# Output projection moved ahead of the last attention unit, residual in a ring of three, q added on GpSimd, ScalarE's order written by hand

## The chip, the cores and the metric

One core of one Trainium2 chip. The time is the device time of one execution in microseconds (us), the median of several. Where two kernels are compared, they ran in turn on the same chip; before had medians of 4112 to 4136 us in five sets of runs, so ratios and not times are compared across sets.

## The reference

Two layers over 32 batches of 512 tokens by 512 features, all float32. The first is attention with 8 heads of 64 under a sparse adjacency mask, the second a graph attention layer over the same mask.

```python
h = relu(layernorm(x));  q, k, v = h @ Wq + bq, h @ Wk + bk, h @ Wv + bv     # 8 heads of 64
attn = softmax(q @ k.T / 8 + (1 - adj) * -1e9);  x = x + (attn @ v) @ Wo + bo
h = relu(layernorm(x));  g = h @ W                                             # layer 2
e = leaky_relu(g @ a[:512] + (g @ a[512:]).T, 0.2) * adj
x = x + elu(softmax(e) @ g + beta * g)
```

## The kernel before

A step of the loop works on four batches at once. Its parts, by letters: units 0 to 3 of the attention of one batch (two heads each: the scores of this unit and the values and sums of the unit before it), V, K, Q, W the four projections (W is the product with Wo), U the combinations of the attention's output oT that W needs (uT), D the sums and diagonal of the second layer's softmax, G its gather, Y its final product, N the transposes of the next batch's normalised x, R the load of the residual.

```python
order = {...}.get(b, "0VDU1G2YNR3WKQ")
```

A projection is done in seven products of quarter size (Strassen's scheme in Winograd's form) and not eight; q is the second of them, and is added to two of the four quarters of the result (abridged: the `yield`s are left out; `one` and `two` are the evictions, which read a finished quarter out of PSUM).

```python
def seven(name, w, B, tokens, one, two):
    ...
    x_ = tile1("x");  times(x_, A11, "b11", True)            # times: sixteen matmuls, 128x256
    y_ = tile1("y");  nc.scalar.copy(y_, x_)
    qz = psum.tile([P, 2, N], F32, ...);  z_ = qz[:, 1, :]
    times(qz[:, 0, :], S1, "t1", True)
    q_ = wtile([P, N], f"q5_{name}", "q5", 1)
    nc.scalar.copy(q_, qz[:, 0, :])                           # q to SBUF
    times(y_, S2, "t2", False, onto=True)
    nc.scalar.copy(z_, y_)                                    # z starts from y
    times(x_, A12, "b21", False, onto=True);   one(0, 0, x_)
    times(z_, S3, "t3", False, onto=True);     two(1, 1, z_, q_)
    times(y_, S4, "b22", False, onto=True);    two(0, 1, y_, q_)
    times(z_, NA22, "t4", False, onto=True);   one(1, 0, z_)
```

TensorE's, VectorE's and GpSimd's order is that of the program text; ScalarE's is found by the compiler. VectorE's work that has time is put into a list with a time from which it may run and a cost; after each TensorE block the program's own clock says what fits.

```python
def pe(us):
    clock["pe"] += us
    while True:
        for i, (key, ready, cost, fn) in enumerate(spare):
            if max(clock["dve"], ready) + cost <= clock["pe"] + 0.4:
                spare.pop(i); clock["dve"] = max(clock["dve"], ready) + cost; fn(); break
        else:
            return

def later(key, wait, cost, fn):
    spare.append((key, max(clock["dve"], clock["pe"]) + wait, cost, fn))
```

On this list are: the statistics and normalisation of the batch that N turns one step later (`norm0`, `x` below; "the next batch's" from here on), the reciprocal of the softmax sums (`rd`), the statistics and dot products of the second layer (of its normalised input `hn`), and the four rows `at` of its softmax. `need(key)` forces what is left of a kind. W adds to the residual:

```python
def add(i, k, p):
    r = x1[k][:, :, ts(i, H)]
    nc.vector.scalar_tensor_tensor(r, quarter(p), 1.0 / VS, r, op0=ALU.mult, op1=ALU.add)
def two(i, k, p, r):
    add(i, k, p)
    add(i, k, r)                     # q, from SBUF
    ...
```

## Time and profile before

| | before |
|---|---|
| median of 3 runs | 4135.91 us (4128.72 to 4138.94) |
| profiled execution | 4131.9 us, granted clock 0.959 |
| one steady step | 126.2 us; 110.9 if TensorE never waited |

TensorE is busy most of the time, so what counts is how much longer each part of a step takes than its matmuls need. A line of the timeline gives start, duration, engine, line, operation, output and inputs, shapes, number. The prediction shows the lines of V, where most is lost.

```profile
2041.62 3.61 PE L502 MATMUL po<-e,v 128*64 128x512 f32 x16
...
2048.60 5.01 PE L472 MATMUL ps<-qT,kT 64*128 64x512 f32 x16
```

The sixteen matmuls of the values take 3.6 us. The sixteen of the scores take 5.0, after the 2.02 us wait for `rd` that the prediction shows.

### The profile page before, as it was taken

The page shows a single profiled execution, that of the slowest core. Times are in us where ns is not written, and L with a number is a line of the kernel's source. Part 1 is how long each engine was busy: PE and PEld are TensorE (multiplying, and loading weights), DVE is VectorE, ACT ScalarE, POOL GpSimd, SP SyncE. Part 2 cuts the span into 40 slices and gives each one's busy share as a digit, 9 for nine tenths or more (in the row PEclk, how much of TensorE's full clock was granted, in tenths as well). Part 3 has the DMA queues.
Part 4 walks back from the last instruction along what each step waited for, and adds up shares of the span by engine and source line. Part 5 has one row for each costly group of instructions (what it writes and reads, how often), then busy time and mean ns, then how long its engine had stood idle before and what let it go on. Part 6 is the DMA issues. An engine that isn't in the chain of part 4 may idle for free. (4 is left out here: it accounts for less than half of the span.)

```text
span 4131.9 us, 59288 instructions
## 1 busy us (share of the span) xinstructions
PE 3762.2 (91%) x24402; PEld 1812.2 (44%) x24402; DVE 2500.7 (61%) x3577; ACT 1400.9 (34%) x2086; POOL 2178.4 (53%) x1762
## 2 busy tenths in 40 slices
PE   8899999999999999999999999999999998999976
PEld 5344444444444444444444444444344444444422
DVE  5566655566656666556666556665556665666563
ACT  3333333333333333333333333333333333333321
POOL 5545556455565455564555644655545556545542
PEclk9899999999999999999999999999999999999988
DMA  3001101001101011010001010111000110101010
GB/s 106 23 3 34 34 31 34 12 25 34 34 31 34 4 34 34 32 34 9 28 34 34 31 34 4 34 34 34 31 17 21 34 34 31 34 4 34 24 33 24
DMA packets 71604, 120.86 MB, mean 29 GB/s; under 512 B 12384, under 2 KB 16480, under 8 KB 71328
## 3 DMA queue, kind: packets, MB, share of 16 engines
q1 hardware_dynamic: 69872, 115.18, 8.8%
q8 instruction: 193, 3.16, 0.3%
q0 software_dynamic: 368, 0.79, 0.1%
q10 hardware_dynamic: 1088, 1.05, 0.1%
q14 instruction: 83, 0.68, 0.1%
HBM read 83.37 MB, written 33.63 MB: 28 GB/s over the span
## 5 line engine op out<-in xcount | busy, mean ns | idle before, releaser
L482 DVE TENSOR_TENSOR e<-ps,nmT 128x1024 f32<-128x1024 f32 x384 | 456.8, 1217 | 667.7 <-PE ps L472 667.6
L493 POOL TENSOR_TENSOR es<-e,e 128x512 f32<-128x512 f32 x256 | 335.4, 1333 | 768.3 <-ACT e L486 768.3
L493 POOL TENSOR_TENSOR es<-es,e 128x512 f32<-128x512 f32 x512 | 693.8, 1387 | 0.0
L486 ACT ACTIVATE e<-e 128x1024 f32<-128x1024 f32 x512 | 541.3, 1057 | 411.0 <-DVE e L482 368.2
L472 PE MATMUL ps<-qT,kT 64*128 64x512 f32 x2048 | 513.8, 644 | 2.7 <-DVE e L482 2.7
L502 PE MATMUL po<-e,v 128*64 128x512 f32 x2048 | 464.2, 594 | 0.4 <-ACT e L486 0.2
L522 DVE RECIPROCAL rd<-pd 128x512 f32<-128x512 f32 x128 | 428.9, 3351 | 41.5 <-POOL oT L525 41.5
L46 PE MATMUL pg<-at,hn 128*64 128x512 f32 x2048 | 449.9, 597 | 4.4 <-DVE dmax L645 2.2
L46 PE MATMUL py<-w,gT 128*64 128x512 f32 x2048 | 446.4, 594 | 0.0
L525 POOL TENSOR_TENSOR oT<-oT,rd 128x512 f32<-128x512 f32 x128 | 168.3, 1315 | 332.4 <-DVE rd L522 332.4
L472 PEld LDWEIGHTS ps<-qT,kT 64*128 64x128 f32 x2048 | 199.7, 202 | 325.7 <-issue 234.2
L283 POOL TENSOR_TENSOR rs<-rs,mhalf 128x2 f32<-128x2 f32 (+1 forms) x96 | 87.6, 913 | 424.8 <-DVE rs L282 392.6
L46 PE MATMUL qz_v<-wv,tT 128*64 128x256 f32 x1024 | 170.8, 493 | 145.7 <-ACT qz_v L387 145.7
L46 PEld LDWEIGHTS pg<-at,hn 128*64 128x64 f32 x2048 | 146.0, 138 | 303.2 <-issue 276.7
L46 PEld LDWEIGHTS py<-w,gT 128*64 128x64 f32 x2048 | 145.1, 137 | 296.9 <-issue 247.6
L502 PEld LDWEIGHTS po<-e,v 128*64 128x64 f32 x2048 | 141.2, 137 | 250.8 <-issue 233.8
L675 POOL TENSOR_TENSOR y<-y,x 128x512 f32<-128x512 f32 x128 | 167.7, 1319 | 158.0 <-DVE y L673 101.6
L672 DVE TENSOR_SCALAR y<-y 128x512 f32<-128x512 f32 x128 | 100.0, 781 | 246.6 <-ACT y L671 246.6
L515 ACT COPY oT<-po 128x512 f32<-128x512 f32 x128 | 74.4, 581 | 514.0 <-PE po L502 514.0
L509 PE MATMUL pd<-es,ones 128*64 128x512 f32 x512 | 151.6, 650 | 78.0 <-DVE rd L522 69.4
L424 POOL TENSOR_TENSOR qT<-qT,edge 128x256 f32<-128x256 f32 x128 | 91.6, 737 | 188.0 <-DVE qT L420 188.0
L671 ACT ACTIVATE y<-py,rd 128x512 f32<-128x512 f32 x128 | 87.9, 687 | 284.7 <-PE py L46 216.6
(180 smaller groups left out, 5939.7 us busy)
## 6 DMA issues: line engine op xcount, KB each, us to landing
x<-in_x_dram SPq DMA_DIRECT2D x128, 256.0 KB, 2.9
x<-in_x_dram SPq DMA_DIRECT2D x64, 512.0 KB, 4.4
out_dram<-y SPq DMA_DIRECT2D x128, 256.0 KB, 2.3
s<-row_s SPq DMA_DIRECT2D x32, 256.0 KB, 3.7
adj<-in_adj_dram SPq DMA_DIRECT2D x4, 256.0 KB, 7.8
w<-in_L_gnn_W_dram SPq DMA_DIRECT2D x1, 1024.0 KB, 7.8
wk<-in_L_gnn_Wk_dram ACTq DMA_DIRECT2D x3, 256.0 KB, 5.0
wq<-in_L_gnn_Wq_dram SPq DMA_DIRECT2D x3, 256.0 KB, 6.4
```

The costliest lines, as they stand in the source:

```text
L46: nc.tensor.matmul(out[s : s + HD], lhsT[:, s : s + HD], rhs, start=start, stop=stop, skip_group_check=onto)
L424: nc.gpsimd.tensor_tensor(qh, qh, edge8[:, ts(k, H)], op=ALU.mult)
L472: nc.tensor.matmul(ps[s], st["kT"][j][rows, ts(k, P)], st["qT"][j][rows, :], start=True, stop=True)
L482: nc.vector.tensor_tensor(e, p, nmT[:, k, :].unsqueeze(1).to_broadcast([P, 2, N]), op=ALU.add)
L486: nc.scalar.activation(e, e, AF.Exp)
L493: nc.gpsimd.tensor_tensor(es[:, s, :], one[:, s, :], e[:, s, :], op=ALU.add)
L502: nc.tensor.matmul(po[s * HD : (s + 1) * HD, :], v[k // 2][:, k % 2, (2 * j + s) * HD : (2 * j + s + 1) * HD], e[k][:, s, :], start=k == 0 ...
L509: nc.tensor.matmul(pd[s * HD : (s + 1) * HD, :], ones[:, :HD], st["es"][j][:, s, :], start=True, stop=True)
L522: nc.vector.reciprocal(rd, st["pd"])
L525: nc.gpsimd.tensor_tensor(o, o, rd, op=ALU.mult)
L672: nc.vector.tensor_scalar(y, y, 1.0, -1.0, op0=ALU.min, op1=ALU.add)
L675: nc.gpsimd.tensor_tensor(y, y, st["x1"][t // 2][:, t % 2, :], op=ALU.add)
```

## The change

Four things at once: W goes ahead of unit 3, so that its results are there sooner; the residual, which W needs, is loaded in two halves at different places, the first ahead of Y, in a ring of three buffers used in turn (paid for by a ring of three in place of four for the attention's output oT); q is added on GpSimd, not VectorE; ScalarE's order is taken from the text, with a second list (`ends`) for ScalarE and GpSimd work that follows deferred VectorE work. Some waits and costs of the list were adjusted too.

```diff
-BY_HAND = {mybir.EngineType.PE, mybir.EngineType.DVE, mybir.EngineType.Pool}
+BY_HAND = {
+    mybir.EngineType.PE, mybir.EngineType.DVE, mybir.EngineType.Pool, mybir.EngineType.Activation,
+}
 ...
+    def then(key, fn):
+        ends.append((key, clock["dve"], fn))      # done by pe() once clock["pe"] + 0.4 has reached it
 ...
-        nc.scalar.copy(q_, qz[:, 0, :])
+        nc.scalar.activation(q_, qz[:, 0, :], AF.Copy, scale=scale)
+        if more:
+            more(q_)
 ...
-            st["o"].append(pair(b, "oT", j // 2, "oP", 4))
+            st["o"].append(pair(b, "oT", j // 2, "oP", 3))
 ...
-    def residual(b, st, tag="x1", bufs=2):            # both halves
+    def residual(b, st, i, tag="x1", bufs=3):         # half i
 ...
             add(i, k, p)
-            add(i, k, r)
 ...
+        def more(q_):
+            for i in (1, 0):
+                r = x1[1][:, :, ts(i, H)]
+                nc.gpsimd.tensor_tensor(r, r, quarter(q_), op=ALU.add)
 ...
-                    later(key, 1.5 + i, 0.7, lambda t=t, g=g, r=r: third(t, g, r))
+                        later(key, 1.2 + i, 0.8, lambda t=t, g=g, r=r: third(t, g, r))
 ...
-            later(("at", b), 5.5, 1.45, lambda k=k: rest(k))
+            later(("at", b), 4.5, 1.6, lambda k=k: rest(k))
 ...
-        norm0(b, states[b]["x"], *((30.0, 10.0) if b > 1 else (6.0, 2.0)))
+        norm0(b, states[b]["x"], *((36.0, 6.0) if b > 1 else (6.0, 2.0)))
 ...
-        }.get(b, "0VDU1G2YNR3WKQ")
+        }.get(b, "0VDU1G2rYNRW3KQ")                   # r: first half of the residual, R: second
```

(The exponential of the last scores, the exponentials and sums of `at`, the ReLUs of `hn` and what follows `rd` are moved into functions given to `then`.)

More of the change, by code (lines that the diff above doesn't have):

```diff
@@ L149, with run_spare @@
     clock = {"pe": 0.0, "dve": 0.0}
-    spare = []
+    spare, ends = [], []
+    def run_spare(i):
+        _, ready, cost, fn = spare.pop(i)
+        clock["dve"] = max(clock["dve"], ready) + cost
+        fn()
     def pe(us):
         clock["pe"] += us
+        till = clock["pe"] + 0.4
         while True:
-            for i, (key, ready, cost, fn) in enumerate(spare):
-                if max(clock["dve"], ready) + cost <= clock["pe"] + 0.4:
-                    spare.pop(i)
-                    clock["dve"] = max(clock["dve"], ready) + cost
-                    fn()
-                    break
+            fits = [i for i, (_, t, cost, _) in enumerate(spare) if max(clock["dve"], t) + cost <= till]
+            due = [i for i, (_, t, _) in enumerate(ends) if t <= till]
+            if due:
+                ends.pop(due[0])[2]()
+            elif fits:
+                run_spare(fits[0])
             else:
@@ L171, in later @@
         spare.append((key, max(clock["dve"], clock["pe"]) + wait, cost, fn))
+    def then(key, fn):
+        ends.append((key, clock["dve"], fn))
     def need(key):
-        while any(k == key for k, *_ in spare):
-            i = next(i for i, (k, *_) in enumerate(spare) if k == key)
-            _, ready, cost, fn = spare.pop(i)
-            clock["dve"] = max(clock["dve"], ready) + cost
-            fn()
+        while True:
+            mine = [i for i, e in enumerate(ends) if e[0] == key]
+            todo = [i for i, e in enumerate(spare) if e[0] == key]
+            if mine:
+                ends.pop(mine[0])[2]()
+            elif todo:
+                run_spare(todo[0])
+            else:
+                return
     adj_sb = []
@@ L354, in turn, with seven @@
         st["hT"] = combos(b, "tT", h)
-    def seven(name, w, B, tokens, one, two):
+    def seven(name, w, B, tokens, one, two, scale=1.0, more=None):
         def times(p, a, bl, start, onto=False):
@@ L485, in scores, with rest @@
             dve(1.2)
-        nc.scalar.activation(e, e, AF.Exp)
         st["e"][j].append(e)
-        if k == 1:
-            st["es"][j] = wtile([P, 2, N], f"es_{b}_{j}", "es", 1)
-        if k:
-            one, es = (st["e"][j][0] if k == 1 else st["es"][j]), st["es"][j]
-            for s in range(2):
-                nc.gpsimd.tensor_tensor(es[:, s, :], one[:, s, :], e[:, s, :], op=ALU.add)
+        def rest():
+            nc.scalar.activation(e, e, AF.Exp)
+            if k == 1:
+                st["es"][j] = wtile([P, 2, N], f"es_{b}_{j}", "es", 1)
+            if k:
+                one, es = (st["e"][j][0] if k == 1 else st["es"][j]), st["es"][j]
+                for s in range(2):
+                    nc.gpsimd.tensor_tensor(es[:, s, :], one[:, s, :], e[:, s, :], op=ALU.add)
+        if k < T - 1:
+            rest()
+        else:
+            then("e", rest)
     def values(b, j, st):
         need("rd")
+        need("e")
         po = st["po"] = psum.tile([P, N], F32, name=f"po_{b}_{j}", tag="po")
@@ L522, in divide, with rest @@
             nc.vector.reciprocal(rd, st["pd"])
-            junk = wtile([P, N], f"rj_{b}_{j}", "rj", 1, BF16)
-            nc.scalar.activation(junk, rd, AF.Copy, accum_out=rsum[:, b, j : j + 1])
-            nc.gpsimd.tensor_tensor(o, o, rd, op=ALU.mult)
-        later("rd", 0.0, 3.4, divide)
-    def residual(b, st, tag="x1", bufs=2):
-        st["x1"] = []
-        for i in range(2):
-            r = pair(b, "x1", i, tag, bufs)
-            nc.sync.dma_start(r, x[b, ts(i, H), :].rearrange("(t p) f -> p t f", p=P))
-            for t in range(2):
-                nc.gpsimd.tensor_tensor(r[:, t, :], r[:, t, :], c_row, op=ALU.add)
-            st["x1"].append(r)
+            def rest():
+                junk = wtile([P, N], f"rj_{b}_{j}", "rj", 1, BF16)
+                nc.scalar.activation(junk, rd, AF.Copy, accum_out=rsum[:, b, j : j + 1])
+                nc.gpsimd.tensor_tensor(o, o, rd, op=ALU.mult)
+            then("rd", rest)
+        later("rd", 0.0, 3.4, divide)
+    def residual(b, st, i, tag="x1", bufs=3):
+        r = pair(b, "x1", i, tag, bufs)
+        nc.sync.dma_start(r, x[b, ts(i, H), :].rearrange("(t p) f -> p t f", p=P))
+        for t in range(2):
+            nc.gpsimd.tensor_tensor(r[:, t, :], r[:, t, :], c_row, op=ALU.add)
+        st["x1"].append(r)
     def out_proj(b, st):
@@ L556, in two @@
             add(i, k, p)
-            add(i, k, r)
             if i == 0:
                 norm1(b, st, (2, 3))
-        return seven(f"w{b}", wo, st["oT"], True, one, two)
+        def more(q_):
+            for i in (1, 0):
+                r = x1[1][:, :, ts(i, H)]
+                nc.gpsimd.tensor_tensor(r, r, quarter(q_), op=ALU.add)
+        return seven(f"w{b}", wo, st["oT"], True, one, two, 1.0 / VS, more)
     def norm1(b, st, rows):
@@ L579, in second, with rest @@
             nc.vector.scalar_tensor_tensor(nb, mv[:, :, 0], -1.0, rstd, op0=ALU.mult, op1=ALU.mult)
-            for i, t in enumerate(rows):
-                hn = wtile([P, D], f"hn_{b}_{t}", "hn", 4)
-                nc.scalar.activation(
-                    hn, st["x1"][t // 2][:, t % 2, :], AF.Relu,
-                    bias=nb[:, i : i + 1], scale=rstd[:, i : i + 1],
-                )
-                st["hn"][t] = hn
-                for g, r in ((0, wa1_r), (1, wa2_r)):
-                    later(key, 1.5 + i, 0.7, lambda t=t, g=g, r=r: third(t, g, r))
+            def rest():
+                for i, t in enumerate(rows):
+                    hn = wtile([P, D], f"hn_{b}_{t}", "hn", 4)
+                    nc.scalar.activation(
+                        hn, st["x1"][t // 2][:, t % 2, :], AF.Relu,
+                        bias=nb[:, i : i + 1], scale=rstd[:, i : i + 1],
+                    )
+                    st["hn"][t] = hn
+                    for g, r in ((0, wa1_r), (1, wa2_r)):
+                        later(key, 1.2 + i, 0.8, lambda t=t, g=g, r=r: third(t, g, r))
+            then(key, rest)
         def third(t, g, r):
@@ L614, in rest, with summed @@
             nc.vector.scalar_tensor_tensor(z, z, ALPHA, z, op0=ALU.mult, op1=ALU.max)
-            nc.scalar.activation(z, z, AF.Exp)
             st["at"].append(z)
-            if k == 1:
-                st["as"] = wtile([P, N], f"as_{b}", "as", 1)
-                nc.gpsimd.tensor_tensor(st["as"], st["at"][0], z, op=ALU.add)
-            elif k > 1:
-                nc.gpsimd.tensor_tensor(st["as"], st["as"], z, op=ALU.add)
+            def summed():
+                nc.scalar.activation(z, z, AF.Exp)
+                if k == 1:
+                    st["as"] = wtile([P, N], f"as_{b}", "as", 1)
+                    nc.gpsimd.tensor_tensor(st["as"], st["at"][0], z, op=ALU.add)
+                elif k > 1:
+                    nc.gpsimd.tensor_tensor(st["as"], st["as"], z, op=ALU.add)
+            then(("at", b), summed)
         for k in range(T):
-            later(("at", b), 5.5, 1.45, lambda k=k: rest(k))
+            later(("at", b), 4.5, 1.6, lambda k=k: rest(k))
     def diagonal(b, st):
@@ L682, in new_state @@
         states[b] = {
-            "x": load(b), "e": [[] for _ in range(NP)], "es": {}, "o": [], "at": [], "g": [], "gT": [],
+            "x": load(b), "e": [[] for _ in range(NP)], "es": {}, "o": [], "x1": [], "at": [], "g": [], "gT": [],
             "dots": 0,
         }
-        norm0(b, states[b]["x"], *((30.0, 10.0) if b > 1 else (6.0, 2.0)))
+        norm0(b, states[b]["x"], *((36.0, 6.0) if b > 1 else (6.0, 2.0)))
     def unit(b, j):
@@ L740, in step @@
             "V": V, "D": lambda: diagonal(b - 2, old), "G": G, "Y": Y, "N": turned, "W": W,
-            "K": K, "U": U, "R": lambda: residual(b - 1, prev, *(("e", 4) if b == B else ())),
+            "K": K, "U": U, "r": lambda: residual(b - 1, prev, 0, *(("e", 4) if b == B else ())),
+            "R": lambda: residual(b - 1, prev, 1, *(("e", 4) if b == B else ())),
             "Q": lambda: run(proj_q(b + 1, nxt)),
-            "c": lambda: value_row(ao, bvr), "r": row_constants,
+            "c": lambda: value_row(ao, bvr), "w": row_constants,
         }
         order = {
-            0: "0V1N2c3rKQ", 1: "0VU1N2R3WKQ", B - 1: "0VDU1G2YRW3", B: "0DUGRWY", B + 1: "DGY",
-        }.get(b, "0VDU1G2YNR3WKQ")
+            0: "0V1N2c3wKQ", 1: "0VU1r2NRW3KQ", B - 1: "0VDU1G2rYRW3", B: "0DUGrRWY", B + 1: "DGY",
+        }.get(b, "0VDU1G2rYNRW3KQ")
         for part in order:
```

## The prediction

> **What bounds the kernel now.** I read the page's busy times first, then the waits of TensorE, then the timeline of one steady step (about 2013 to 2140 us), engine by engine.
>
> ```profile
> PE 3762.2 (91%) x24402; PEld 1812.2 (44%) x24402; DVE 2500.7 (61%) x3577; ACT 1400.9 (34%) x2086; POOL 2178.4 (53%) x1762
> ```
>
> TensorE is the bound on average, but 91% hides that matmuls overlap and that some run slowly. The waits say what it waits for (us in total, times, longest):
>
> ```profile
> PE qz_v L46 <- ACT qz_v L387: 145.7, 29, 5.0
> PE pd L509 <- DVE rd L522: 69.4, 33, 9.4
> ...
> PE qz_k L46 <- DVE x L547: 24.1, 19, 1.3
> PE qz_w L46 <- ACT qz_w L387: 20.6, 29, 2.4
> ```
>
> For the true cost I take start-to-start times. An undisturbed block of sixteen 128x256 matmuls takes 1.727 us (Q: 2001.16, 2002.89, 2004.62, ...), so a seven-block projection 12.09. A step is 126.63 us (values at 2013.25 and again at 2139.88). Without gaps it would be 4 projections 48.4, values and sums 4 x 4.39, scores 4 x 3.63, gather 13.8, final 13.9, transposes 1.9, the small sum 0.9: 110.9. So 15.7 us of a step are lost: V (2021.27 to 2040.74, 19.47 for 12.09) 7.4; unit 1 after it 3.9; unit 3 about 0.6; W 1.8; K 2.0; Q 0. V, in order of time:
>
> ```profile
> 2026.91 1.90 PE L46 MATMUL x_v<-wv,hT 128*64 128x256 f32 x16
> ...
> 2029.20 1.75 DVE L611 SCALAR_TENSOR_TENSOR at<-s,s,adjT 128x512 f32<-128x512 f32 x1
> ...
> 2032.65 0.63 ACT L615 ACTIVATE at<-at 128x512 f32<-128x512 f32 x1 [2.71 <-DVE at L614]
> ...
> 2033.19 0.58 ACT L387 COPY qz_v<-y_v 128x512 f32<-128x512 f32 x1
> ...
> 2033.82 3.35 PE L46 MATMUL qz_v<-wv,tT 128*64 128x256 f32 x16 [5.02 <-ACT qz_v L387]
> ```
>
> The 0.58 us copy stands in ScalarE's queue behind the exponentials of `at`, which wait for VectorE; TensorE waits 5 us and then runs at half pace. In unit 1 the reciprocal starts only after the diagonal's VectorE work:
>
> ```profile
> 2043.85 3.35 DVE L522 RECIPROCAL rd<-pd 128x512 f32<-128x512 f32 x1
> ...
> 2047.25 1.42 PE L509 MATMUL pd<-es,ones 128*64 128x512 f32 x4 [2.02 <-DVE rd L522]
> ```
>
> **What the skill says.** "SBUF — State Buffer", Who interferes with whom: a VectorE instruction with two SBUF inputs contends with a GpSimd instruction that reads SBUF, and so does a two-port VectorE one; one blocks the other outright. The trace agrees: the `at` instructions take 0.75 and 0.69 us while GpSimd is idle and 1.75 and 1.63 beside its sums; the add of q from SBUF in W took up to 4.14 against 0.69 from PSUM. "TensorE: Matmul & The Clock Gate", Architectural detail, calls ScalarE and VectorE strict FIFO: the copy above behind work that isn't ready is that. Its Part 1 has the array at half clock after too idle a window: the first block after the 5 us wait took 3.13 us start to start in place of 1.73.
>
> **The change part by part.** The kernel places deferred VectorE work by its own clock: at each TensorE block, what ends within 0.4 us of the block's end is issued, first in the list first. I replayed that arithmetic by hand. For the old order it gives just what the trace has (four `x` statistics, then six dot products before q's first eviction; one `at` before unit 0's scores, three in V), so I trust it for the new order, counted from the end of Y as 0:
> - *W before unit 3.* N ends at 2.4, W at 14.5, unit 3 at 22.5, K at 34.6, Q at 46.7. W's last statistics come in unit 3, `nb` may not come before 21.5 and lands in K; the eight dot products fill K, the last comes at 35.3 in Q. `at` is ready at 40.8, but the statistics of the next `x` stand first in the list and q's evictions take the rest: 45.67 against a limit of 45.38, 47.38 against 47.11. No `at` fits in Q. Unit 2's reciprocal (3.4) fits nowhere in K or Q either and is forced at the start of unit 0. There it pushes all `at` behind the scores: three in V, the fourth forced at the diagonal. Before, one was done ahead of V.
> - *ScalarE by hand.* In V each exponential follows its `at` in that order, so the copy `z<-y` now waits for one `at` in place of three. `at` starts 3 to 4.5 us into V; one pair takes 3.4 beside the sums, so the copy is done at 7.7 to 9.1 and the block starts at 7.9 to 9.3 in place of 6.9: 1.0 to 2.4 lost, not 5.2. But the third `at` stands ahead of the eviction that frees the last block (1.2 to 1.5 lost), and the fourth, with its exponential (0.63) and sum on GpSimd (1.28), ahead of the diagonal (2.8 to 3.3). V: 5.3 to 7.1 in place of 7.4. Unit 1's reciprocal is still forced after the diagonal: 3.9 as before.
> - *Unit 0.* The forced reciprocal starts after q's last eviction, 1.1 us after Q, ends at 4.45; `pd` is due at 3.43: 1.05 lost, new.
> - *Residual early.* It puts 2 adds (1.27 each) ahead of the last sums and of Y's adds on GpSimd, which in Y had no slack:
>
> ```profile
> 2084.21 2.70 POOL L675 TENSOR_TENSOR y<-y,x 128x512 f32<-128x512 f32 x2
> ...
> 2089.72 0.69 ACT L671 ACTIVATE y<-py,rd 128x512 f32<-128x512 f32 x1 [3.12 <-DMA out_dram<-y]
> ```
>
> The fourth `y` takes the first one's buffer, and started 4.2 us after the first add ended (2085.5). With that add at 88.1 it starts at about 92.1 and not 89.5. The two ReLUs that free W's PSUM follow it: W starts at 93.85 in place of 91.1: 2.7 lost.
> - *q on GpSimd.* VectorE loses two adds a step (mean 1.96 us of the group below), GpSimd gains two of about 1.3. Its chain then: fourth y add 95.5, three combinations (1.34) 99.5, residual 102.1, uT 103.4, product with rd 104.7, first q add 106.0. VectorE's eviction ends at 106.7; TensorE's last block of W, due at 104.2, starts at 106.9: 2.7 lost. The change's order W straight after Y is already in the last full step, where it cost 2.0:
>
> ```profile
> L547 DVE SCALAR_TENSOR_TENSOR x<-q_w,x 128x512 f32<-128x512 f32 x64 | 125.3, 1958 | 2.2
> ```
>
> ```profile
> 3980.48 0.69 DVE L547 SCALAR_TENSOR_TENSOR x<-qz_w,x 128x512 f32<-128x512 f32 x1 [3.17 <-POOL x L536]
> ...
> 3981.72 1.95 PE L46 MATMUL qz_w<-wo,uT 128*64 128x256 f32 x16 [1.88 <-POOL uT L333]
> ```
>
> - *K.* The old wait for the q add goes. But four `hn` activations (0.80 each) now stand ahead of the q copy (1.1 lost), and the dot products run beside unit 3's sums at about 1.7 in place of 0.69, ahead of an eviction (1.1 to 2.1 lost): 2.3 to 3.3.
>
> **The sum.** After: unit 0 1.05, V 5.3 to 7.1, unit 1 3.9, N and W 5.4, unit 3 0, K 2.3 to 3.3: 18 to 20.8, about 19 if I shade it for waits that overlap. Before: 15.7. So 3 us more a step, 29 full steps: 4136 + 90 = 4226, say 4220.
>
> **Rivals.** (1) The order by hand does what it is meant to: V loses 1 us as in the last full step, where `at` came early and V and unit 1 had next to no stall; the trade is 6 us in V, perhaps 3.5 in unit 1, against 3 in W: 3 to 6 us a step, 3960 to 4050. For it: the 5 us wait is the largest by far and is aimed at. Against: the replayed order, which leaves `at` in V. (2) Gains and new waits cancel: V wins 3 and the rest gives back 2 to 4: 4100 to 4170. For it: GpSimd is 53% busy, so its backlog may be shorter than my chain. (3) GpSimd becomes the bound from Y to W and new gaps of 2 to 3 us each also cost half clock (1.7 each as in V and unit 1): 6 or 7 us more a step, 4310 to 4340. For it: from unit 2's first sum (2076.6) to the first q add it has 25.7 us of work (6 sums, 4 residual adds, 4 y adds, 3 combinations, uT, product and q, each at 1.25 to 1.34), and TensorE only 24.9 to the block that waits for it (2101.5).
>
> **Range and chances.** The replay of order I hold for likely right; the durations under contention are the soft part, plus or minus 3 us a step, or 90 us, and an error of 0.3 us in the replay would move an `at` into Q and bring rival 1 nearer. Range 4070 to 4320. Faster by over 2% (under 4053): 0.17; within 2%: 0.38; slower by over 2% (over 4219): 0.45.
>
> **What would show it.** Right: TensorE's wait for ScalarE's `z<-y` falls to 1 to 2.5 us in place of 5.0; a wait of some 1 us for `rd` in unit 0; a wait of 2 to 3 us for W's first block behind ReLU, and for its last behind x; a wait of the diagonal's sum for `as`; q add on GpSimd ending 12 us after W starts; dot products at over 1 us mean. Wrong: if `at` appears in Q, if unit 1's `pd` no longer waits, or if W runs in 12.1 us with no gap, the time is below 4100.

## The result, and the profile after

| | before | after |
|---|---|---|
| median (4 runs each, same rounds) | 4135.67 us | 4154.19 us (4152.32 to 4155.69) |
| ratio of fast runs | 1 | 1.0047, 95% interval 1.0029 to 1.0064 |
| one steady step | 126.19 us | 126.62 us |

A ratio is the mean time of one kernel's fast runs over that of the other's of the same rounds, so not quite the ratio of the medians. The kernel is 0.5% slower: a large change moved the time by next to nothing.

To see where it went I took from the trace the starts of the matmuls and worked out, for every part of a step, the time from its first matmul to the first of the next part, as a mean over 28 steady steps. Less the time without waits, this is what a part loses (us a step; parts that lose under 0.05 left out, as G, Y, unit 2 and Q are in both):

| part | without waits | before loses | after loses | predicted for after |
|---|---|---|---|---|
| unit 0 | 8.02 | 0.0 | 1.15 | 1.05 |
| V | 12.09 | 7.8 | 5.8 | 5.3 to 7.1 |
| D | 0.88 | 0.0 | 0.1 | (in V) |
| unit 1 | 8.02 | 3.9 | 2.3 | 3.9 |
| N | 1.89 | 0.0 | 1.2 | 2.7 |
| W | 12.09 | 2.0 | 2.3 | 2.7 |
| unit 3 | 8.02 | 0.35 | 0.1 | 0 |
| K | 12.09 | 1.3 | 2.8 | 2.3 to 3.3 |
| sum | | 15.3 | 15.7 | 18 to 20.8 |

The page's busy times of after, to be set beside the first line of the prediction:

```profile
PE 3700.6 (89%) x24402; PEld 1845.2 (44%) x24402; DVE 2555.8 (62%) x3513; ACT 1390.7 (34%) x2086; POOL 2301.1 (55%) x1826
```

VectorE has 64 instructions fewer (the q adds) and is busy for longer all the same: its others met GpSimd more often, above all the dot products (302.9 us in place of 167.3, lines under dots_late). What TensorE waits for (us in total, times, longest):

```profile
PE pe L49 <- POOL as L660: 131.6, 31, 23.8
PE qz_w L49 <- DVE x L576: 61.1, 30, 5.5
PE qz_k L49 <- DVE kT L460: 54.4, 30, 1.8
PE pd L536 <- DVE rd L549: 46.9, 56, 1.1
PE qz_v L49 <- ACT qz_v L406: 45.1, 29, 1.6
PE x_w L49 <- ACT hT L365: 31.8, 29, 2.8
```

The old wait for ScalarE's `z<-y` has shrunk from 145.7 to 45.1 us, as it was meant to. In its place stand a wait at the diagonal for GpSimd's sum of `at` (3.05 us a step), one for `rd` in two units and not one (56 times, at most 1.1 us each), and new ones at W's first and last block and in K. One step from V to unit 1, in order of time:

```profile
2038.75 0.63 ACT L655 ACTIVATE at<-at 128x512 f32<-128x512 f32 x1 [3.19 <-DVE at L651]
2039.29 0.58 ACT L406 COPY qz_v<-y_v 128x512 f32<-128x512 f32 x1
2039.92 1.95 PE L49 MATMUL qz_v<-wv,tT 128*64 128x256 f32 x16 [1.55 <-ACT qz_v L406]
...
2045.35 1.64 DVE L651 SCALAR_TENSOR_TENSOR at<-at 128x512 f32<-128x512 f32 x1
2047.02 0.63 ACT L655 ACTIVATE at<-at 128x512 f32<-128x512 f32 x1 [0.33 <-DVE at L651]
2049.11 1.22 PE L49 MATMUL pe<-ones,as 128*64 128x64 f32 x16 [3.05 <-POOL as L660]
2050.12 4.61 PE L529 MATMUL po<-e,v 128*64 128x512 f32 x16
2055.78 1.08 PE L536 MATMUL pd<-es,ones 128*64 128x512 f32 x4 [1.04 <-DVE rd L549]
2056.78 3.70 PE L491 MATMUL ps<-qT,kT 64*128 64x512 f32 x16
```

The copy now stands behind one exponential of `at`, and costs 1.55 us. But all four `at` are still here, the last in front of D. Read the last four lines against those of before: the values now run slowly (4.61 for 3.61) and the scores at full pace (3.70 for 5.01). The second half of the change, from N to W:

```profile
2095.59 1.56 SPq L717 DMA_DIRECT2D out_dram<-y  x2
...
2097.70 0.69 ACT L712 ACTIVATE y<-py,rd 128x512 f32<-128x512 f32 x1 [3.88 <-DMA out_dram<-y]
...
2099.41 1.95 PE L49 MATMUL x_w<-wo,oT 128*64 128x256 f32 x16 [1.00 <-ACT hT L365]
...
2109.93 2.49 POOL L592 TENSOR_TENSOR x<-x,q_w 128x512 f32<-128x512 f32 x2
2111.23 0.69 DVE L576 SCALAR_TENSOR_TENSOR x<-qz_w,x 128x512 f32<-128x512 f32 x1 [3.88 <-POOL x L592]
2111.97 1.95 PE L49 MATMUL qz_w<-wo,uT 128*64 128x256 f32 x16 [1.98 <-DVE x L576]
```

The fourth `y` waits for the store of the first, the ReLUs and so W's first block wait for it; W's last block waits for the eviction of z, which waits for GpSimd's first q add, which comes 10.5 us after W's start.

### The profile page after: what moved, and what is told of

It reads as the page before. It is cut to its first block, busy times and chain, and to the rows that moved or that the text cites. A ratio compares the mean times of both kernels' runs of the same rounds, so it can differ in the third digit from the quotient of the medians.

```text
span 4150.1 us, 59223 instructions
## 1 busy us (share of the span) xinstructions
PE 3700.6 (89%) x24402; PEld 1845.2 (44%) x24402; DVE 2555.8 (62%) x3513; ACT 1390.7 (34%) x2086; POOL 2301.1 (55%) x1826
## 3 DMA queue, kind: packets, MB, share of 16 engines
q10 hardware_dynamic: 1088, 1.05, 0.1%
## 4 chain that ended last, share of the span: by engine, by line
PE 40%; DVE 30%; POOL 15%; issue 8%; ACT 4%; DMA 2%; DVEq 0%; ACTq 0%; POOLq 0%; SPq 0%
PE pg L49 11%; PE po L529 6%; DVE e L501 5%; PE ps L491 5%; POOL es L514 5%; DVE rd L549 5%; PE qz_q L49 4%; DVE at L651 4%; DVE at L648 3%; DVE scr L629 3%; PE pd L536 3%; POOL x L565 3%; DVE e L498 3%; PE y_q L49 3%; PE x_q L49 3%
## 5 line engine op out<-in xcount | busy, mean ns | idle before, releaser
L514 POOL TENSOR_TENSOR es<-es,e 128x512 f32<-128x512 f32 x512 | 734.9, 1460 | 3.0 <-ACT e L508 2.9
L529 PE MATMUL po<-e,v 128*64 128x512 f32 x2048 | 508.9, 640 | 17.2 <-ACT e L508 17.0
L491 PE MATMUL ps<-qT,kT 64*128 64x512 f32 x2048 | 475.6, 603 | 2.8 <-DVE e L501 2.7
L300 POOL TENSOR_TENSOR rs<-rs,mhalf 128x2 f32<-128x2 f32 (+1 forms) x96 | 77.5, 807 | 509.9 <-DVE rs L299 509.7
L629 DVE CUSTOM_DVE_ANT_0 scr<-hn,wa_r 128x512 f32<-128x512 f32 x256 | 302.9, 1227 | 61.2 <-ACT hn L617 61.2
L491 PEld LDWEIGHTS ps<-qT,kT 64*128 64x128 f32 x2048 | 184.7, 186 | 291.3 <-issue 191.1
L553 ACT ACTIVATE rj<-rd 128x512 bf16<-128x512 f32 x128 | 80.7, 630 | 635.2 <-DVE rd L549 635.0
L529 PEld LDWEIGHTS po<-e,v 128*64 128x64 f32 x2048 | 162.2, 150 | 293.1 <-issue 260.6
L49 PE MATMUL qz_k<-tT,wk 128*64 128x256 f32 x1024 | 126.2, 388 | 73.8 <-DVE kT L460 54.4
```

The costliest lines, as they stand in the source:

```text
L49: nc.tensor.matmul(out[s : s + HD], lhsT[:, s : s + HD], rhs, start=start, stop=stop, skip_group_check=onto)
L491: nc.tensor.matmul(ps[s], st["kT"][j][rows, ts(k, P)], st["qT"][j][rows, :], start=True, stop=True)
L514: nc.gpsimd.tensor_tensor(es[:, s, :], one[:, s, :], e[:, s, :], op=ALU.add)
L529: nc.tensor.matmul(po[s * HD : (s + 1) * HD, :], v[k // 2][:, k % 2, (2 * j + s) * HD : (2 * j + s + 1) * HD], e[k][:, s, :], start=k == 0 ...
L629: nc.vector.tensor_tensor_reduce(scr, st["hn"][t], r, 1.0, 0.0, op0=ALU.mult, op1=ALU.add, accum_out=st["s12"][:, g, t : t + 1],)
```

## The experiments

**Theory A**: the order by hand is a large gain, and it is hidden because the new order of parts, the early residual and the q adds create the waits above. What fills V in after is VectorE's deferred work: the next batch's statistics stand in Q and its normalisations in unit 0 and early in V, push the `at` behind them, and the fourth lands ahead of D. **Theory B**, with its variants: the order by hand is worth little in itself, or W is limited by something that none of these parts sets. In the expectations, A and B are what the two say of the point at hand. Twelve kernels ran, each correct. All stage times below are worked out as in the table above.

| run | what it is | median us | ratio to before, 95% | step us |
|---|---|---|---|---|
| hand_only | before with ScalarE's order by hand | 3882.91 | 0.9428 (0.9412 to 0.9443) | 119.3* |
| hand_q_on_G | the same, q added on GpSimd | 3993.38 | 0.9659 (0.9638 to 0.968) | 121.1 |
| W_back | after with W after unit 3 again | 4040.95 | 0.9813 (0.9797 to 0.9829) | 122.7 |
| q_on_DVE | after with q on VectorE again | 4085.44 | 0.9921 (0.9905 to 0.9938) | 124.4 |
| act_auto | after with ScalarE's order by the compiler | 4335.68 | 1.0549 (1.052 to 1.0578) | 133.0 |
| norm_in_G | after, next batch's norm due in G | 3926.03 | 0.953 (0.9514 to 0.9546) | 118.5 |
| dots_late | after, dot products due later | 4097.94 | 0.9967 (0.9939 to 0.9995) | 124.8 |
| at_12 | after, `at` taken as 1.2 us | 4204.48 | one run, no ratio | 128.3 |
| r_in_G | after, first half of residual before G | 4145.01 | 1.0028 (1.0003 to 1.0053) | 126.3 |
| hand_psum_q | hand_only, q read from PSUM | 3927.64 | 0.9501 (0.9478 to 0.9524) | 118.7 |
| best1 | hand_psum_q with norm_in_G | 3785.01 | 0.9157 (0.9135 to 0.918) | 113.5 |
| best2 | best1, both q adds at the first eviction | 3752.33 | 0.9132 (0.9109 to 0.9155) | 112.5 |

*The profiled run of hand_only was its slow one (3939 us; the others 3876 to 3884), so its step and stages are those of a slow run.

### hand_only and act_auto: ScalarE's order by hand

hand_only is after with the old order of parts, both halves of the residual after N in a ring of two, oT's ring of four and q on VectorE; of the four parts of the change it keeps the order by hand (with the second list and the adjusted waits and costs, which no run separates from it in the old order of parts).

```diff
-        }.get(b, "0VDU1G2rYNRW3KQ")
+        }.get(b, "0VDU1G2YNrR3WKQ")
-            st["o"].append(pair(b, "oT", j // 2, "oP", 3))
+            st["o"].append(pair(b, "oT", j // 2, "oP", 4))
-    def residual(b, st, i, tag="x1", bufs=3):
+    def residual(b, st, i, tag="x1", bufs=2):
             add(i, k, p)
+            add(i, k, r)                                  # and no more()
```

> ScalarE's order by hand alone: W after the last attention unit, the residual at its old place with a ring of two, Wo's q on VectorE, as in the kernel before. Theory A (the order by hand is worth several us a step and the other three parts give it back): V from 19.9 to 13-15 us, unit 1 10-12, W and K together 26-27; a step of 120-122 us, the kernel at 3970-4030 us, faster than both. Theory B (the order by hand itself trades one wait for another, the other parts are neutral): V stays over 17 us and the kernel within 1.5% of 4135.

Measured: 0.9428, so 5.7% faster than before, more than expected. V falls from 19.9 to 14.1 us. Theory A's first half holds. act_auto is the mirror image: after with ScalarE left out of BY_HAND, the adjusted waits and costs kept.

> The changed kernel with ScalarE's order left to the scheduler as before, all else changed. Tells what the order by hand is worth in the new order of parts. Theory A (it is worth as much here as alone, some 235 us, and the other three parts cost 255): V over 21 us, ratio 1.04-1.07. Theory B (in the new order the exponentials stand late in any case, so the hand order is worth little): ratio 0.995-1.02.

It is 1.0549, so the order by hand, and it alone, is worth 5.0% in the new order of parts (1.0549 over 1.0047). V takes 22.9 us, and the wait that the order by hand was made for is back (waits of TensorE in act_auto):

```profile
PE qz_v L49 <- ACT qz_v L406: 128.3, 29, 4.4
```

### q_on_DVE, W_back and hand_q_on_G: the other three parts

q_on_DVE takes `more` out of after and puts `add(i, k, r)` back.

> The changed kernel with Wo's q added on VectorE again. Theory A (GpSimd's chain of y, combinations, residual, uT, product, q sets the end of W, its last block waits 2.0 us for it): W falls from 14.4 to 12.5-13.3 us, K and the rest stay within 0.5 us; 4105-4135 us. Theory B (VectorE's add of q from SBUF is blocked by GpSimd for up to 4 us as in the kernel before, so it was right to move it): W stays at 14 or over, or unit 3 and K get longer by as much; 4150-4190 us.

W shrinks from 14.42 to 12.20 us and nothing else moves much; the time is lower than expected. Adding q on GpSimd costs 1.3% in the new order. W_back is after with only the order of parts put back ("0VDU1G2YNrR3WKQ").

> The changed kernel with Wo (and both halves of the residual) back behind the transposes and the last attention unit in the old order: N, residual, unit 3, W, K, Q. Tells what the new place of W costs. Theory A: N 1.9 in place of 3.1 (GpSimd's early residual adds no longer delay y), unit 0 8.0 in place of 9.2 (unit 2's reciprocal finds a place in W), V 13-15 in place of 17.9 because two `at` come ahead of unit 0's scores, but W 14-15 (the q add waits for the sums of unit 3 on GpSimd); a step of 121-123, the kernel at 3990-4060 us. Theory B (W's new place is worth something by itself): slower than 4154.

V (13.3) and N (1.9) came as expected, but W took 19.0 us. Two lines of its timeline say why:

```profile
2051.77 0.59 ACT L542 COPY oT<-po 128x512 f32<-128x512 f32 x1 [7.75 <-PE qz_w L49]
...
2055.74 3.36 PE L49 MATMUL y_w<-wo,uT 128*64 128x256 f32 x16 [4.02 <-ACT y_w L395]
```

With a ring of three, the copy of this unit's output into oT must wait until W has read the buffer, 7.75 us, and the copy that W itself needs stands behind it, and behind three exponentials, on ScalarE. So this run undid one part and met the price of another: a ring cut from four to three is harmless only where W comes early. To separate the two, and to see q's move alone, hand_q_on_G has the old order of parts with oT's ring of four, the residual's ring of two, and q on GpSimd:

```diff
-            st["o"].append(pair(b, "oT", j // 2, "oP", 3))
+            st["o"].append(pair(b, "oT", j // 2, "oP", 4))
-    def residual(b, st, i, tag="x1", bufs=3):
+    def residual(b, st, i, tag="x1", bufs=2):
-        }.get(b, "0VDU1G2rYNRW3KQ")
+        }.get(b, "0VDU1G2YNrR3WKQ")
```

> The order by hand in the old order of parts, as in hand_only, with the one more part that q is added on GpSimd; residual, its ring of two and oT's ring of four as before. It tells whether q's move costs by itself or only in the new order. Theory A: the cost in the new order (2.2 us a step) comes from GpSimd's full chain between the final stage and W; where W stands after unit 3 and GpSimd has the time of a unit ahead of it, q's move costs little in W (12.2 to 13.5 us there) and takes the lock on q away in K (12.1 us in every step, and not 12.1 or 15 to 18): step 117 to 119, ratio to before 0.93 to 0.945. Theory B, q on GpSimd costs wherever it stands, because the two adds come ahead of the work that W's evictions wait for: W 14.0 to 15 us, ratio 0.95 to 0.965.

My theory A fell here. q's move costs 2.4% (0.9659 over 0.9428), more than in the new order, and W took 17.5 us, worse than either theory had it. Timeline of hand_q_on_G:

```profile
2031.78 2.49 POOL L592 TENSOR_TENSOR x<-x,q_w 128x512 f32<-128x512 f32 x2
2033.08 0.69 DVE L576 SCALAR_TENSOR_TENSOR x<-qz_w,x 128x512 f32<-128x512 f32 x1 [5.89 <-POOL x L592]
2033.83 3.68 PE L49 MATMUL qz_w<-wo,uT 128*64 128x256 f32 x16 [4.69 <-DVE x L576]
```

The q adds stand in GpSimd's order behind unit 3's sums, the product of oT with `rd` and uT; VectorE's eviction of z waits for them, and TensorE for the eviction, and then the block takes 3.68 us and not 1.95. The four corners together:

| ratio to before | q on VectorE | q on GpSimd |
|---|---|---|
| W after unit 3, oT's ring of four | 0.9428 | 0.9659 |
| W after unit 3, oT's ring of three, residual's of three | not run | 0.9813 |
| W ahead of unit 3, residual half early | 0.9921 | 1.0047 |

So of the change's parts one wins 5.7% and two give it back: W's place with what it brings (4.9 points with q on VectorE, 3.9 on GpSimd), and q's move (1.3 or 2.3).

### norm_in_G: why W's place costs so much

The prediction had replayed the list: with W ahead of unit 3 the second layer's `at` become due in Q, where the statistics of the next batch stand first. norm_in_G leaves everything of after and makes those due later, after the `at`, in G, where VectorE had time.

```diff
-        norm0(b, states[b]["x"], *((36.0, 6.0) if b > 1 else (6.0, 2.0)))
+        norm0(b, states[b]["x"], *((72.0, 3.0) if b > 1 else (6.0, 2.0)))
```

> The changed kernel with one number changed: the next batch's layer norm becomes due 72 us after the transposes and not 36, so it falls into the gather (G), where VectorE is idle for 14 us, and no longer into Q. Theory A (the next batch's statistics push `at` out of Q and unit 0 into V, and that one displacement makes the waits of V, of the diagonal's sum, of unit 1's and of unit 0's reciprocal): three `at` come ahead of unit 0's scores, V falls from 17.9 to 12.1-12.5 us, unit 1 from 10.3 to 8.0, unit 0 from 9.2 to 8.0, a step from 126.6 to about 117.5, the kernel to 3870-3910 us. Theory B (the order on ScalarE by hand or VectorE's amount of work is the limit, not the place of `at`): V stays over 15 us or the waits move into G, and the time stays within 2% of 4154.

In every step three `at` now start ahead of V and one in it; in after all four started in V. V fell from 17.9 to 12.3, D from 1.0 to 0.9, unit 1 from 10.3 to 8.1, unit 0 from 9.2 to 8.1: all without a wait, or nearly. N, W and K kept theirs, as they should. The step was 118.5 where 117.5 was expected, W a little longer, and the time 3926, a little above the expected range. The wait at the diagonal, formerly in every step, is left twice in the whole run (waits of TensorE in norm_in_G):

```profile
PE pe L49 <- POOL as L660: 42.1, 2, 23.6
```

One pair of numbers is thus worth 5.1% (0.953 over 1.0047): W's new place was not bad in itself, it had moved work into a window that was already full.

### dots_late: K

```diff
-                        later(key, 1.2 + i, 0.8, lambda t=t, g=g, r=r: third(t, g, r))
+                        later(key, 7.0 + i, 0.8, lambda t=t, g=g, r=r: third(t, g, r))
```

> The changed kernel with the dot products due 7 us after their `hn` and not 1.2. Theory A (in K they run beside unit 3's sums on GpSimd at 1.7 us in place of 0.7, ahead of the evictions, and that is K's wait of 1.8 us as well as what pushes the reciprocal and `at` back): the dot products' mean falls from 1.23 to 0.7-0.8 us, K from 14.85 to 12.5-13.1, unit 0 from 9.2 to 8.0-8.5, V to 13-15 with two `at` ahead of unit 0's scores, unit 1 up to 11-12; a ratio of 0.955-0.975. Theory B (later dot products only make `at` later still): V and the diagonal's wait grow, ratio over 1.0.

The groups of the dot products (count, busy us, mean ns of one, idle before them) in before, after and dots_late:

```profile
L592 DVE CUSTOM_DVE_ANT_0 scr<-hn,wa_r 128x512 f32<-128x512 f32 x256 | 167.3, 700 | 0.9 <-ACT hn L582 0.9
```

```profile
L629 DVE CUSTOM_DVE_ANT_0 scr<-hn,wa_r 128x512 f32<-128x512 f32 x256 | 302.9, 1227 | 61.2 <-ACT hn L617 61.2
```

```profile
L629 DVE CUSTOM_DVE_ANT_0 scr<-hn,wa_r 128x512 f32<-128x512 f32 x256 | 170.9, 707 | 2.7 <-ACT hn L617 2.7
```

In after they run beside GpSimd's sums of unit 3 and take 1227 ns; put later they take 707 again, and K falls from 14.85 to 12.84, unit 0 to 8.0. That half held. The other half, that V would fall to 13 to 15, did not: V took 17.3 and unit 1 rose to 11.65. Of the four `at` two now start ahead of V in about half of the steps and one in the others, but the next batch's normalisations, which the later dot products had pushed on, in V together with the other two. It is the same displacement once more with another victim, and the run is only 0.8% below after.

### at_12: unit 1

Here I made the list take an `at` for shorter than it is, so that more of them go ahead of the diagonal.

```diff
-            later(("at", b), 4.5, 1.6, lambda k=k: rest(k))
+            later(("at", b), 4.5, 1.2, lambda k=k: rest(k))
```

> The changed kernel with 1.2 and not 1.6 as the assumed cost of one `at`: one goes into Q, the fourth into V, so the diagonal's sum no longer waits; unit 2's and unit 3's reciprocals stay forced where they were. Tells the half clock from the wait in unit 1. Theory A (in the changed kernel the diagonal's 3 us wait starts the half-clock stretch early, so that the values run slowly while the reciprocal is computed and the scores run at full pace; in the kernel before the stretch began at the reciprocal's wait and fell on the scores): the wait before the diagonal goes, but the wait for the reciprocal grows from 1.0 to about 2.0 and unit 1 from 10.3 to 11-12 us. Theory B (unit 1 is shorter in the changed kernel for another reason): unit 1 stays at 10.3 or less.

Timeline of at_12 from the diagonal on:

```profile
2074.35 3.61 PE L529 MATMUL po<-e,v 128*64 128x512 f32 x16
2080.00 1.08 PE L536 MATMUL pd<-es,ones 128*64 128x512 f32 x4 [2.04 <-DVE rd L549]
2081.01 5.40 PE L491 MATMUL ps<-qT,kT 64*128 64x512 f32 x16
```

The wait at the diagonal is gone in steady steps (131.6 to 40.8 us in all). And unit 1 became longer, 11.7 for 10.3 us: it looks as in before again, values at full pace, 2 us of wait, scores at half pace. In after the wait for the sum of `at` comes first, the slow matmuls behind it are the values, and the values run while VectorE's reciprocal runs: their slowness is hidden behind a wait that would be there anyway. It is one run, but its steps test the pairing again: in 25 of 29 the scores take 4.8 to 5.4 us and unit 1 11.9 to 12.0, in the other four the scores behind the same wait run at full pace, and unit 1 takes 10.3, just what it is in after. One of these four:

```profile
2462.84 3.61 PE L529 MATMUL po<-e,v 128*64 128x512 f32 x16
2468.48 1.08 PE L536 MATMUL pd<-es,ones 128*64 128x512 f32 x4 [2.03 <-DVE rd L549]
2469.49 3.70 PE L491 MATMUL ps<-qT,kT 64*128 64x512 f32 x16
```

So the 1.6 us between before and after in unit 1 are the slow scores, and a slow stretch is paid only where nothing else covers it. Why the same wait is not always followed by one is worked out under r_in_G.

### r_in_G: N

```diff
-        }.get(b, "0VDU1G2rYNRW3KQ")
+        }.get(b, "0VDU1rG2YNRW3KQ")
```

> The changed kernel with the early half of the residual one unit earlier, ahead of the gather, where GpSimd is idle for some 14 us. Theory A (the two early adds delay GpSimd's y adds by 2.5 us, hence the fourth y, the ReLUs and W's start, and the chain to the q add): N from 3.1 to 1.9, W from 14.4 to 12.5-13.7; 2 to 3 us a step, 4040-4080 us on a chip that runs the kernel before in 4116. Theory B (the chain is held up by the fourth y or the DMA of the second half, not by GpSimd's amount of work): N and W together stay within 0.5 us of 17.5.

N lost nothing any more (1.95), so the early half's two adds on GpSimd were the cause of its 1.2 us. But W lost 0.5 more, unit 3 0.25, and the time stayed. The timeline of r_in_G:

```profile
2349.64 1.28 POOL L716 TENSOR_TENSOR y<-y,x 128x512 f32<-128x512 f32 x1 [2.14 <-issue]
...
2359.74 2.49 POOL L592 TENSOR_TENSOR x<-x,q_w 128x512 f32<-128x512 f32 x2
...
2361.78 3.59 PE L49 MATMUL qz_w<-wo,uT 128*64 128x256 f32 x16 [1.96 <-DVE x L576]
```

W starts at 2349.24 here. The fourth `y` add begins 0.40 us later and the q adds 10.50 us later; in after it is 0.43 and 10.52. What lies between is the same serial chain on GpSimd (the add, three combinations, the residual's second half, uT, the product with `rd`), and it moves with Y's end, not with the residual's first half. TensorE's wait at the end is equal too (1.96 and 1.98), but the block behind it took 3.59 us here and 1.95 in after. Over the 29 full steps it took 1.95 in 12 and 2.5 to 3.6 in the other 17; in after it took 1.95 in 26 of 29. The granted clock tells why. In the steady part of these traces it is 1.0 or 0.5, and the stretches of 0.5 are 3.41 us or a multiple, with starts whole multiples of 3.41 us apart: a fixed grid. The grid around W's wait, first in after and then in r_in_G (from and to, length, TensorE busy and instructions, granted clock, DMA share, GB/s):

```profile
2106.76:2110.17 3.41, 3.23 (x30) 1.00 0.11 42
2110.17:2113.58 3.41, 1.61 (x16) 1.00 0.00 0
```

```profile
2358.51:2361.92 3.41, 1.45 (x16) 1.00 0.00 0
2361.93:2365.34 3.41, 3.41 (x18) 0.50 0.00 0
```

Between 600 and 3700 us of after, the 28 windows of this grid that came just before a slow stretch held 1.96 to 2.77 us of idle TensorE (by the profile's modelled ends of matmuls), the 833 others at most 1.96; in r_in_G it is 39 with 1.95 or more and 810 with at most 1.95. So in these runs what counts is how much of a wait falls within one window. In after the wait straddles an edge (0.18 and 1.80 us idle), and as a step is 126.3 us, 37 windows, in 24 of 29 steps, it falls there again and again. In r_in_G a step has another length, the wait often lies within one window, and W pays: the 1.1 us won in N are lost for the larger part. norm_in_G's W (14.3 to 16.0 us from step to step) shows such slow blocks too.

### hand_psum_q, best1 and best2: a version that beats both

If q costs on VectorE (two SBUF inputs, shut out by GpSimd) and costs on GpSimd (a late place in its order), it can stay in PSUM, where VectorE reads it as one of its inputs. hand_psum_q is hand_only with

```diff
+        if keep:
+            q_ = qz[:, 0, :]
+        else:
             q_ = wtile([P, N], f"q5_{name}", "q5", 1)
             nc.scalar.activation(q_, qz[:, 0, :], AF.Copy, scale=scale)
```

> ScalarE's order by hand alone (as hand_only), but Wo's q is read by VectorE straight from PSUM and not from a copy in SBUF, so that the add has one SBUF input. Theory A (what made K 12.1 us in some steps and 15 to 18 in others was that the add of q, with two SBUF inputs, was shut out by GpSimd for up to 5.4 us): L576's adds all take about 0.7 us, K is 12.1 us in every step, W stays at 12.2; some 3 us a step less than hand_only's profile, 3790-3840 us. Theory B (the delay is in GpSimd's queue or in the order, not in the port): K keeps its 15-18 us in half of the steps, 3870-3900 us.

K took 12.09 us in every step: the shut-out is gone (in before K is 13.4; hand_only's 15.4 is from its slow run). But W took 13.94 and the time was 3928, not the 3790 to 3840 that I had expected, and not below hand_only's. best1 adds norm_in_G's edit to it.

> Order by hand, q from PSUM, and the next batch's layer norm in G; everything else as in the kernel before. If the three losses add up as the parts did: V 12.1-12.5, unit 1 8.0-8.3, W 12.2, K 12.1, a step of 111.5-113 us against 110.9 without any wait; 3690-3740 us, 10% faster than before. If another engine takes over (VectorE has 85 us of work a step in contended form), 3760 or more.

It is 8.4% faster than before, not the 10% expected; what is missing is W, again 13.94. Timeline of best1:

```profile
1935.25 0.69 DVE L579 SCALAR_TENSOR_TENSOR x<-qz_w,x 128x512 f32<-128x512 f32 x1
...
1936.08 1.95 PE L49 MATMUL qz_w<-wo,uT 128*64 128x256 f32 x16 [1.61 <-POOL es L517]
```

The wait is put down to GpSimd's `es` (a sum of exponentials), which the block does not read. What ends just ahead of it is VectorE's second reading of q (1935.25 plus 0.69 is 1935.94). q and z are halves of one PSUM tile, so I took it that the last product into z waits for the last reading of q; `es` ends within 0.1 us of it, so only a run can tell. best2 does both q adds right after the first eviction of z:

```diff
             add(i, k, p)
-            add(i, k, r)
+            if i == 1:
+                add(1, k, r)
+                add(0, k, r)
```

> As best1, but VectorE reads both halves of q from PSUM at the first eviction, so that W's last block no longer waits for the second reading of the same PSUM tile. Theory A (that late reading is the 1.8 us of W in hand_psum_q and best1): W from 13.94 to 12.3-12.7 us, all else as in best1, a step of 111.7-112.2, a ratio to before of 0.903-0.909. Theory B (W's last block waits for GpSimd's uT or the sums, as the waits name it): W stays at 13.9.

W fell to 12.87 and the step to 112.5 us, 1.6 above the 110.9 without waits, so the reading of q was most of that wait. The ratio is 0.9132, the lowest of all but above the expected 0.903 to 0.909, and its interval overlaps best1's.

## Why the prediction was right or wrong

The time came out at 4154, inside the range and 66 us below the 4220 named; of the three outcomes the most likely one was put at slower by over 2%, and what happened is 0.5% slower.

**The order replayed was right** in what was checked: no `at` in Q or unit 0, the fourth ahead of the diagonal, `rd` forced at the start of unit 0, seven of eight dot products in K beside unit 3's sums, q's chain on GpSimd behind W. norm_in_G shows that this displacement is the cause, not a companion, of the stalls from unit 0 to unit 1.

**Terms that were right in size**: unit 0 (1.05, measured 1.15), V (5.3 to 7.1, measured 5.8; of its three waits the one ahead of the last block, put at 1.2 to 1.5, was 0.7), K (2.3 to 3.3, measured 2.8), W's end (2.7, measured 2.3), unit 3 (0, measured 0.1).

**The first term mis-sized is unit 1**, "3.9 as before". It measured 2.3. I carried over a number of before that held a wait and a slow stretch behind it, without asking whether the slow stretch would still stand where it is paid. The change put a 3 us wait ahead of the values, the slow stretch moved onto the values, and these run beside the reciprocal. From the diagonal's sum to `pd` it is 6.51 us before (2040.74 to 2047.25) and 6.67 after (2049.11 to 2055.78), but the scores behind take 3.70 and not 5.01. at_12 turned it back.

**The second is N**, 2.7, measured 1.2. I took the time for a `y` buffer to come free from before, 4.2 us from the end of the first `y` add to the fourth exponential, because the profile put that wait down to the store. In the step that I read this was so, but that step was an odd one. The first store and the fourth exponential of it, and of the next step (before):

```profile
2085.70 1.58 SPq L676 DMA_DIRECT2D out_dram<-y  x2
...
2089.72 0.69 ACT L671 ACTIVATE y<-py,rd 128x512 f32<-128x512 f32 x1 [3.12 <-DMA out_dram<-y]
```

```profile
2212.36 1.57 SPq L676 DMA_DIRECT2D out_dram<-y  x2
...
2216.06 0.69 ACT L671 ACTIVATE y<-py,rd 128x512 f32<-128x512 f32 x1 [2.80 <-POOL y L675]
```

In the first the store landed 3.92 us after its issue, in the second after 2.05; it is 2.0 to 2.1 in 23 of before's 29 full steps. In 25 of the 29 the exponential began 3.7 us after the issue and 0.1 us after its own matmuls, which ended last: the buffer had mostly been free for 1.6 us. In after, where the buffer is last, the store was issued at 2095.59 and the exponential began at 2097.70: 2.1 us. r_in_G confirmed that the early adds are the cause. Reading one more step would have shown it.

Together these two are 1.6 and 1.5 us a step, 3.1 us, or 90 us over 29 steps: as much as the whole of the predicted slowdown. So these two terms are what failed in the prediction: "unit 1 still 3.9", where the slow stretch was assumed to stay on the scores, and W's start at 93.85, where a store's time was taken from one odd step. The waits themselves came where it put them. **Of the rivals** the second, that gains and new waits cancel (4100 to 4170), is what happened, though not for its reason (a shorter backlog on GpSimd: W's chain was as long as worked out). The first, that the order by hand does what it is meant to, is what the change would have given without its other parts: hand_only is below even that rival's 3960 to 4050. I had judged the change as one thing and did not ask what each part would give alone.

**What stays open**: which of W's place, the residual's early half and the ring of three makes up how much of the 4.9 points with q on VectorE (r_in_G and norm_in_G say that most is the displacement, W_back and hand_q_on_G that the two rings of three, oT's by the timeline, cost 1.6% in the old order), how much of hand_only's 5.7% is the adjusted waits and costs (one pair of such numbers was worth 5.1% in norm_in_G; act_auto gives 5.0% for the order alone, in the new order of parts), and why one run of hand_only was 1.5% slower than its others.

## What to carry to other kernels

Where deferred work is placed by time, moving one block moves everything that is due after it: before moving it, list what will be due in each window and whether it fits, and give what can wait the window with slack. A wait taken from a trace is the later of two conditions, so a duration read across it holds only while the same condition stays last, and one step may be an odd one. Where a wait brings a slow clock by a fixed grid, a microsecond won elsewhere can move the wait on that grid and be lost again (r_in_G): look at many steps, not one. Judge a bundle part by part: here one part won 5.7%, two gave it back, and the whole showed 0.5%.

## What the Trainium skill lacked or had wrong

- "SBUF — State Buffer", Who interferes with whom, says that whoever issues first has the shared port pair for its whole instruction and the other blocks. The loser can be shut out for more than one instruction: before's add of q, 0.69 us alone, took 4.13 to 4.17 us in 19 steps, beside three GpSimd instructions of some 1.3 us each that followed one another without a gap, and ended only after the third.
- "TensorE: Matmul & The Clock Gate", Part 1, ties half clock to an idle window of about 3.4 us and calls the window free-running. The grid of 3.41 us fits that, but the window needn't be idle throughout: 1.96 to 2.77 us of idle TensorE in it were followed by half clock in after, and at most 1.96 us were not (r_in_G: 1.95 and 1.95).
- No page says what a slow stretch costs where it is put: in after it fell on the values (4.61 us for 3.61) beside the reciprocal and cost nothing; in before and at_12 on the scores, and cost up to 1.7 us (5.40 for 3.70).
